# A two-stage sequence kernel on one core: quartered Wq and Wk loads, the adapter's residual turned into the product's bank, x^T added by GpSimd

## The chip, the cores and the metric

The kernel runs on one core of one Trainium2 chip. The metric is the device time of one execution in microseconds. Three runs of the kernel before took 1192.78, 1194.61 and 1195.8 us; the median is 1194.61. The profile is of one further execution, which took 1194.26 us; the span that the profiler shows for its instructions is 1192.5 us.

## What is computed

Four sequences of 512 tokens with 512 features, all in fp32:

```
q, k, v  = x @ Wq, x @ Wk, x @ Wv
attn_out = softmax(q k^T / sqrt(512)) @ v @ Wp + bp
cms      = gelu(attn_out @ cW1 + cb1) @ cW2 + cb2 + one_hot(code)
modifier = gelu(concat(attn_out, cms) @ mW1 + mb1) @ mW2 + mb2
y        = clip(x + cms + modifier, 0, 1)
# adapter, with weights chosen for each sequence by `stream`
h        = gelu(y @ W_down + b_down) @ W_up + b_up
out      = layernorm(y + h) * ln_w + ln_b
```

cW1 is 512 x 2048, cW2 2048 x 512, mW1 1024 x 2048, mW2 2048 x 512; W_down is 512 x 256 and W_up 256 x 512 for each of three experts.

## The kernel before

The four sequences are taken in two pairs. Nearly every product is cut into halves both ways and done with seven products of half size in place of eight (Strassen-Winograd); the large layers do so at two levels, so that an inner product has 128x128 blocks against 256 columns. The sums of blocks that this needs are made on VectorE for the operands, and on GpSimd for the weights. The sums of weights are made once, written to DRAM (`c1_inner`, `c1_outer`, `c2_kept`, `m1_kept`, `m2_kept`) and fetched by SyncE into four buffers `wslot`.

The order of the work is: the head (Wq and Wk turned, and their product W_qk = Wq Wk^T made by `folded`), then for each pair the attention (`pair_product`, `softmax`, `small_product`), and then for each pair the layers c1, c2, m1, m2 (`c1_layer`, `second_layer`, `m1_layer`, `second_layer`) and the adapters. The adapters of the first pair are taken in small steps beside the second pair's c1 layer; those of the last pair run at the end, where sequence 3 goes first and sequence 2 last.

The instructions of an engine stand in the order that a scheduler gives them from the program's order and its own costs; some are held to the program's order by `keep_in_program_order`. Each engine works its queue in order. A buffer that is written again waits for its readers.

The parts that the change touches:

- Head, L123 to L140 and L801 to L805. `weight` loads Wq and Wk in four DMAs of 128 rows each, of 256 KB, taken in turn from SyncE's and ScalarE's queues; x of sequence 0 and Wv follow on ScalarE's queue, x of sequence 1 and Wp on SyncE's. `transposed` turns a whole matrix: 16 transposes into four PSUM banks; then `left_from_psum` and `right_from_psum` copy each bank (ScalarE, L681 and L641) and make the four sums of blocks (VectorE, L516 and L505). `folded` then does the seven products (order 1, 5, 6, 2, 7, 3, 4) of 4 matmuls each, after that x^T of sequence 0 is turned, the biases are turned (`load_bias`, L157), and x^T of sequence 1 is turned with the operands of the first pair product (`both_operands`).
- GpSimd's work in the first 320 us is `expansion`, the sums of weights, with `left_sums` of x (L178 to L181) in between. `late_expansion` does mW2 beside the first pair's m1 layer.
- `second_operands` makes the operands of c2 and m2 from the four blocks of the hidden layer: t1 = h12 - h11, t3 = h22 - h12, t2 = h22 - t1, t4 = h21 - t2, each in a lower and an upper half (`differences`, 128 x 2048 elements, on VectorE). t3 and t4 overwrite h12 and h11. `after(p, g)` is called when product p of the layer before is done for the half g.
- The end of m1, L1418: x^T, kept in DRAM by the attention stage, is added to `cms` by an accumulating DMA from GpSimd's queue for each sequence.
- The adapter, L1293 to L1370. For each sequence: 16 transposes bring y into rows, four banks `res_ps`, ScalarE copies them (L1317) and GpSimd adds b_up (L1318); `down_ps` is two products of 4 matmuls with a gelu each (L1330); then for each of four row tiles two matmuls into `up_ps` (L1335), and VectorE adds the rows (L1343), takes statistics (L1345, L1347), ScalarE takes the root (L1350), and scale and shift follow on ScalarE, VectorE and GpSimd (L1352 to L1368), and a store.

Of the kernel before, what the change touches and what calls it, by code (L numbers as in the profile page):

```python
# [18 lines left out]
def kernel(  # L19
# [103 lines left out]
    wq = weight((nc.sync, nc.scalar, nc.sync, nc.scalar), Wq, slot[0])  # L123
    wk = weight((nc.sync, nc.scalar, nc.sync, nc.scalar), Wk, slot[1])
# [12 lines left out]
    x_rows = [load_x(0, nc.scalar, x_places[0])]  # L137
    wv = weight((nc.scalar, nc.scalar), Wv, slot[2])
    x_rows.append(load_x(1, nc.sync, x_places[1]))
# [34 lines left out]


# [22 lines left out]


# [17 lines left out]
    def expand_c1(u, then):  # L217
# [23 lines left out]
        yield  # L241

# [43 lines left out]
    def expand(unit, raw, pairs, last, then):  # L286
# [46 lines left out]
        else:  # L333
# [3 lines left out]
            yield from plain((1, a11, two), (4, a22, one))  # L337
            yield from full((5, one), (7, three), (6, two))
            then()

    def expand_all(units, raw, pairs, last):
        if last is None:
            load_raw(*units[0][:2], units[0][3], raw)
        for n, unit in enumerate(units):

            def then():
                if n + 1 < len(units):
                    load_raw(*units[n + 1][:2], units[n + 1][3], raw)

            yield from expand(unit, raw, pairs, last, then)  # L350
# [19 lines left out]
    def late_expansion():  # L370

        yield from expand_all(m2_units, slot[6:8], (flat(mod[0]), flat(mod[1]), slot[0]), None)
# [38 lines left out]
    def transposed(get, dst, finish=None):  # L411

        ps = [bank("tr_ps") for d in range(4)]
# [5 lines left out]
        for d in range(4):  # L419
            if finish is None:  # L420
                evacuate(dst[:, d, :], ps[d])
            else:
                finish(d, ps[d])
# [228 lines left out]
    def small_product(lhs, rhs, keep, then=None, copy=nc.scalar.copy):  # L652


        def matmuls(p, _, ps, first_):
# [14 lines left out]
            (1, 5, 6, 2, 7, 3, 4), then, copy,  # L670
# [5 lines left out]
    def left_from_psum(t, s):  # L676

        s1, s2, s3, s4 = (s[:, k] for k in range(4))

        def finish(d, ps):  # L680
            nc.scalar.copy(t[:, d, :], ps)  # L681
            c = d % 2
            if d < 2:
                minus(s3[:, c], ps[:, :256], t[:, c, 256:])
            else:
                minus(s2[:, c], ps[:, 256:], s3[:, c])
                add(s1[:, c], ps[:, 256:], t[:, c, 256:])
                minus(s4[:, c], ps[:, :256], s2[:, c])

        return finish  # L690

    def folded(lhs, rhs, w, s):
# [17 lines left out]
        small_product(lhs, rhs, keep)  # L710
# [71 lines left out]
    def first_operand(pair):  # L782
        xT, t_x = places(pair)
        transposed(chunks(x_rows[2 * pair]), xT[0], right_from_psum(xT[0], sums_in(flat(t_x[0]))))
# [17 lines left out]
    transposed(chunks(wq), wq_t, left_from_psum(wq_t, s_q))  # L802
    transposed(chunks(wk), wk_t, right_from_psum(wk_t, t_k))
    lhs_qk = folded(left_operand(wq_t, s_q), right_operand(wk_t, t_k), w_qk, sums_in(slot[0]))
    first_operand(0)  # L805
    load_bias()
    begun = both_operands(0)
    for pair in range(B // 2):
# [59 lines left out]
        if pair == 0:  # L868
            begun = {}
            then = {6: [lambda: first_operand(1)], 4: [lambda: begun.update(both_operands(1))]}  # L870
# [89 lines left out]
    def c1_operands(slots=(0, 1, 2, 3)):  # L960

        at0, at1, t12, t34 = (in_rows[i] for i in slots)
        b11, b12, b21, b22 = at0[:, 0:2, :], at1[:, 0:2, :], at0[:, 2:4, :], at1[:, 2:4, :]
        t1, t2, t3, t4 = t12[:, 0:2, :], t12[:, 2:4, :], t34[:, 0:2, :], t34[:, 2:4, :]

        def inner_sums(k, t):
            s = mod[1][:, 2 * k : 2 * k + 2, :].rearrange("p a (b n) -> p (a b) n", b=2)
            return inner_operands(t, 1, [s[:, i : i + 1, :] for i in range(4)], pinned=True)
# [4 lines left out]
        one = {1: inner_sums(0, b11)}  # L973
        minus(t1, b12, b11)

        def rest():
            one[5] = inner_sums(1, t1)
# [6 lines left out]
        return one, {2: b21, 3: b22, 4: t4, 6: t2, 7: t3}, rest()  # L984
# [5 lines left out]
    def c1_two_level(p, h, rhs):  # L990
# [3 lines left out]
        for g in range(2):  # L994
            w = next_weights()
            if p == 1:
                for m in range(2):
                    at = m * 512 + g * 256
                    fetch(
                        out=w[:, 512 * m : 512 * m + 512].rearrange("p (c n) -> p c n", c=2),  # L1000
                        in_=cW1[0:256, at : at + 256].rearrange("(c p) n -> p c n", p=P),
                    )
                fetch(out=w[:, 1024:], in_=c1_inner[1, g])
            else:
                fetch(out=w, in_=c1_inner[5, g])
# [17 lines left out]
        def keep(g, place, ps):  # L1023
            o, t = place
            tiles, tokens = slice(4 * o + 2 * g, 4 * o + 2 * g + 2), slice(256 * t, 256 * t + 256)
            nc.scalar.copy(h[2 if p == 1 else 3][:, tiles, tokens], halves_of(ps))
            if p == 1:
                done = h[0][:, tiles, tokens]
                add(done, halves_of(ps), done)
# [5 lines left out]
    def c1_layer(h, rhs, after):  # L1035

        two_level, one_level, rest = rhs
        for p in FIRST_C:
            if p in (1, 5):
                c1_two_level(p, h, two_level[p])  # L1040
                yield
                continue
            for g in range(2):
                w = next_weights()
                if p in (2, 4):
                    k, o = {2: (1, 0), 4: (1, 1)}[p]
# [9 lines left out]
                else:  # L1056
                    s = {3: 2, 6: 0, 7: 1}[p]
                    a = w[:, :1024].rearrange("p (j c n) -> p j c n", j=2, c=2)
                    for j in range(2):
                        fetch(out=a[:, j], in_=c1_outer[j][:, s, g])  # L1060
                    lhs = lambda c, t, a=a: a[:, t // 2, c, (t % 2) * P : (t % 2 + 1) * P]
                for t in range(4):
                    ps = bank(f"c1_{p}")
                    for c in range(2):
                        nc.tensor.matmul(  # L1065
                            ps, lhsT=lhs(c, t), rhs=one_level[p][:, c, :],
# [89 lines left out]
    def second_operands(h):  # L1156
# [19 lines left out]
        def after(p, g):  # L1176

            if (p, g) == (3, 1):
                differences(1, LOW)
                differences(3, LOW)  # L1180
# [4 lines left out]

        ready = []
        return operands, differences, after, ready

    def second_layer(made, src, kept_w, c, last, bias_c, beside):

        operands, differences, _, ready = made
        c11, c12, c21, c22 = c
        rhs = ready[0]
        for i, p in enumerate(SECOND):
# [3 lines left out]
            if i == 0:  # L1198
# [317 lines left out]
```

## Time and profile before

| | |
|---|---|
| median of 3 runs | 1194.61 us |
| profiled execution, its own time | 1194.26 us |
| its span | 1192.5 us |
| TensorE matmuls busy | 1168.9 us, 98% |
| VectorE | 883.5 us, 74% |
| GpSimd | 482.7 us, 40% |
| ScalarE | 294.9 us, 25% |
| chain that ended last | TensorE 92%, DMA 3%, VectorE 2%, GpSimd 2%, ScalarE 1% |
| DMA | 251.50 MB, mean 211 GB/s |
| granted TensorE clock | 0.997 of full |

Times in the profile are microseconds from the start of the span unless they are marked ns. PE is TensorE's matmuls and PEld its weight loads, DVE is VectorE, ACT ScalarE, POOL GpSimd and SP SyncE; a name with a q is the sequencer of that engine, which issues DMAs and waits. A row names the line of the kernel, the engine, the operation, what is written and read, its size and how often; in brackets stands the idle time before it and what ended that. An fp32 matmul shows as two records, a transpose as one. A busy engine costs time only where it is on the chain that ends last; TensorE is on it nearly everywhere, so the question for each stage is whether TensorE stops there and for what.

### The profile page before, as it was taken

Reading aid. Unit: us, or ns where it says so; the run is one execution under the profiler, and the core shown is the slowest. Engines: PE = TensorE matmul, PEld = TensorE weight load, DVE = VectorE, ACT = ScalarE, POOL = GpSimd, SP = SyncE. Lnnn points to the kernel's source line nnn. Section 1 sums busy time; section 2 is a strip of 40 time slices with the busy share of each in tenths; the row PEclk is TensorE's granted clock in tenths of the full one; section 3 lists DMA queues with packets and bytes.
Section 4 is the critical chain, followed back from the end, with each engine's and each line's share of the span. In section 5 each row is a group of like instructions: output and inputs, shape, how many; then the busy total and the mean of one; then the engine's idle time right before and its main releaser. Section 6 shows DMA issues by size and latency. Waiting matters only on the chain.

```text
span 1192.5 us, 13167 instructions
## 1 busy us (share of the span) xinstructions
PE 1168.9 (98%) x4809; PEld 894.8 (75%) x4809; DVE 883.5 (74%) x1221; ACT 294.9 (25%) x540; POOL 482.7 (40%) x542
## 2 busy tenths in 40 slices
PE   7999999999999999999999999999999999999996
PEld 6478558747468888888888857447888888888872
DVE  4735565476789867897899837779894588699947
ACT  3234325335520000012310037551000002220014
POOL 4788999988940048870000522110000010124015
PEclk9999999999999999999999999999999999999998
DMA  8743695698756478787737553132735454775601
GB/s 289 277 149 135 245 351 196 218 389 331 262 194 249 176 279 319 283 293 251 241 134 297 177 177 133 54 132 106 293 131 187 166 211 168 219 240 187 228 1 71
DMA packets 78368, 251.50 MB, mean 211 GB/s; under 512 B 7348, under 2 KB 34016, under 8 KB 63456
## 3 DMA queue, kind: packets, MB, share of 16 engines
q1 hardware_dynamic: 54768, 149.96, 35.0%
q0 software_dynamic: 20736, 89.17, 21.2%
q10 hardware_dynamic: 2800, 11.54, 2.5%
q8 instruction: 38, 0.62, 0.2%
q14 instruction: 26, 0.21, 0.1%
HBM read 185.63 MB, written 65.01 MB: 210 GB/s over the span
## 4 chain that ended last, share of the span: by engine, by line
PE 92%; DMA 3%; DVE 2%; POOL 2%; ACT 1%; SPq 1%; issue 0%; ACTq 0%; DVEq 0%; POOLq 0%
PE i L1215 28%; PE i L1131 27%; PE c L1065 10%; PE sum L595 8%; PE sum L659 7%; PE sum L1014 4%; PE down_ps L1323 2%; PE up_ps L1335 2%; DMA wslot<-c_inner 1%; DMA wslot<-in_L_cond_mW 1%; PE tr_ps L416 1%; PE prod_ps L430 1%; PE res_ps L1314 1%; DMA wide<-in_L_cond_Wk 1%; SPq L988 1%
## 5 line engine op out<-in xcount | busy, mean ns | idle before, releaser
L1131 PE MATMUL i<-slot,wslot 128*128 128x256 f32 x1184 | 260.8, 379 | 0.0
L1131 PEld LDWEIGHTS i<-slot,wslot 128*128 128x128 f32 x1184 | 225.0, 190 | 30.6
L1215 PE MATMUL i<-slot,wslot 128*128 128x256 f32 x896 | 202.5, 379 | 0.0
L1215 PEld LDWEIGHTS i<-slot,wslot 128*128 128x128 f32 x896 | 170.2, 190 | 23.1
L906 ACT COPY first<-i 128x256 f32<-128x256 f32 (+1 forms) x56 | 26.8, 479 | 544.9 <-PE i L1215 280.6
L1215 PE MATMUL i<-hidden,wslot 128*128 128x256 f32 x576 | 132.2, 379 | 0.0
L899 DVE TENSOR_TENSOR part<-i,part 128x512 f32<-128x512 f32 (+1 forms) x156 | 90.9, 591 | 43.1 <-PE i L1131 26.6
L1215 PEld LDWEIGHTS i<-hidden,wslot 128*128 128x128 f32 x576 | 109.4, 190 | 16.2 <-issue 1.4
L928 ACT ACTIVATE hidden<-hidden,bias 128x512 f32<-128x512 f32 x128 | 85.2, 716 | 61.8 <-DVE hidden L505 60.7
L1065 PE MATMUL c<-slot,wslot 128*128 128x512 f32 x224 | 97.3, 592 | 0.0
L1065 PEld LDWEIGHTS c<-slot,wslot 128*128 128x128 f32 x224 | 42.5, 190 | 53.1 <-issue 50.5
L1286 POOL DMA_INDIRECT slot<-in_L_cond_W_down,idx_d x12 | 15.5, 1288 | 149.8 <-PE i L1215 88.2
L1286 POOL DMA_INDIRECT slot<-in_L_cond_b_up,idx_e x3 | 4.3, 1420 | 174.1 <-PE i L1131 173.5
L505 DVE TENSOR_TENSOR sum<-sum,wslot 128x512 f32<-128x512 f32 x51 | 35.4, 697 | 36.8 <-PE sum L659 18.7
L190 DVE TENSOR_TENSOR slot<-hidden,slot 128x1024 f32<-128x1024 f32 x48 | 58.4, 1217 | 0.3
L190 DVE TENSOR_TENSOR slot<-hidden 128x1024 f32<-128x1024 f32 x48 | 58.4, 1216 | 0.0
L899 DVE TENSOR_TENSOR part<-i,first 128x512 f32<-128x512 f32 (+1 forms) x62 | 36.3, 589 | 28.6 <-PE i L1131 16.2
L505 DVE TENSOR_TENSOR hidden<-c,hidden 128x512 f32<-128x512 f32 x64 | 43.3, 688 | 15.5 <-PE c L1065 14.3
L659 PE MATMUL sum<-hidden,wslot 128*128 128x256 f32 x232 | 53.5, 380 | 0.4 <-POOL wslot L180 0.4
L284 POOL DMA_DIRECT2D slot<-in_L_cond_mW x24 | 17.9, 753 | 81.4 <-DVE slot L190 80.5
L659 PEld LDWEIGHTS sum<-hidden,wslot 128*128 128x128 f32 x232 | 43.6, 190 | 6.8 <-POOL wslot L180 0.8
L505 DVE TENSOR_TENSOR hidden<-part,hidden 128x2048 f32<-128x2048 f32 x20 | 48.1, 2405 | 0.5
(307 smaller groups left out, 1988.6 us busy)
## 6 DMA issues: line engine op xcount, KB each, us to landing
wslot<-m_kept SPq DMA_DIRECT2D x48, 1024.0 KB
wslot<-m_kept SPq DMA_DIRECT2D x36, 512.0 KB
wslot<-c_kept SPq DMA_DIRECT2D x16, 1024.0 KB
slot<-in_L_cond_mW POOLq DMA_DIRECT2D x24, 512.0 KB
wslot<-in_L_cond_mW SPq DMA_DIRECT2D x24, 512.0 KB
slot<-in_L_cond_cW POOLq DMA_DIRECT2D x16, 512.0 KB
wslot<-in_L_cond_cW SPq DMA_DIRECT2D x32, 256.0 KB
m_kept<-wide POOLq DMA_DIRECT2D x6, 1024.0 KB
```

What stands on the lines that cost most here:

```text
L190: i = eng.tensor_tensor(out_, one, two, ALU.subtract)
L505: nc.vector.tensor_tensor(dst, a, b, ALU.add)
L595: nc.tensor.matmul(ps, lhsT=lhs[p][:, c, r * P : (r + 1) * P], rhs=rhs[p][:, c, :], start=(first_ and c == 0), stop=(c == 1), skip_group_c ...
L659: nc.tensor.matmul(v[:, j, :], lhsT=lhs[p][:, c, j * P : (j + 1) * P], rhs=rhs[p][:, c, :], start=(first_ and j == 0 and c == 0), stop=(c ...
L899: nc.vector.tensor_tensor(dst, ps, other, ALU.add)
L906: nc.scalar.copy(c1, p1)
L928: nc.scalar.activation(block[:, t, :], block[:, t, :], AF.Gelu, bias=bias_c[:, 8 * half + t : 8 * half + t + 1],)
L1014: nc.tensor.matmul(halves_of(ps)[:, j, :], lhsT=a[g][:, at_[q], j * P : (j + 1) * P], rhs=rhs[q][:, 0, :], start=(first_ and j == 0), stop ...
L1065: nc.tensor.matmul(ps, lhsT=lhs(c, t), rhs=one_level[p][:, c, :], start=(c == 0), stop=(c == 1),)
L1131: nc.tensor.matmul(out_ps[:, j, :], lhsT=a[j][q][:, c, :], rhs=now[q][:, c, :], start=(c == 0), stop=(c == 1),)
L1215: nc.tensor.matmul(ps[:, :256], lhsT=a[k // 2][q][:, k % 2, :], rhs=now[q][:, k, :], start=(k == 0), stop=(k == 3),)
L1323: nc.tensor.matmul(ps, lhsT=wd[:, c, n * P : (n + 1) * P], rhs=y[:, c, :], start=(c == 0), stop=(c == NV - 1),)
```

## The change

Six things change; the diff below is cut to their core.

Head: Wq and Wk are loaded in quarters (256 rows by 256 columns, 256 KB each), Wq's on SyncE's queue and Wk's on ScalarE's; x of sequences 0 and 1, Wv and Wp all follow on SyncE's queue. Fifteen products of a tile of zeros are put ahead on TensorE, and a copy of one column (`touched`) ahead on ScalarE. Each pair of quarters is turned by 8 transposes; product 1 comes after the first pair, the other pairs after product 1, in `folded`, whose order is now 1, 2, 5, 6, 7, 3, 4. The sums are made on 512 columns at a time. x^T of sequence 0 is turned after product 6, and its evacuation follows product 7.

`second_operands`: except in the first pair's c1 layer (`busy`), the lower half of t1 is made of two negations on ScalarE and an accumulating DMA of h12 from GpSimd's queue, and the lower half of t3 follows at the start of the next layer.

c1: the sums for the two products at two levels (p = 1 and 5) are made inside `c1_layer` and no longer before it.

Expansion: in `expand` for mW2, the next unit's loads are asked for before the last three groups of sums, and three steps instead of two go beside each step of m1.

x^T: it is loaded into a buffer (slot 3) and added to `cms` by four GpSimd additions for each sequence, for the first sequence of the pair already inside m1.

Adapter: b_up is gathered as columns and added to y^T by ScalarE (`with_bias`); y^T with it is turned into the bank of the up product, to which the two matmuls are added. Statistics and the first scaling read the bank. The last sequence's down product is cut into token halves, and two row tiles go up before the last quarter of it.

```diff
+    def quarters(src, dst, eng):
+        w = dst.rearrange("p (c n) -> p c n", c=4)
+        for r, k in QUARTERS:
+            rows, columns = slice(256 * r, 256 * r + 256), slice(256 * k, 256 * k + 256)
+            eng.dma_start(
+                out=w[:, 2 * r : 2 * r + 2, columns],
+                in_=src[rows, columns].rearrange("(c p) n -> p c n", p=P),
+            )
+        return w
+    QUARTERS = ((0, 0), (0, 1), (1, 0), (1, 1))
-    wq = weight((nc.sync, nc.scalar, nc.sync, nc.scalar), Wq, slot[0])
-    wk = weight((nc.sync, nc.scalar, nc.sync, nc.scalar), Wk, slot[1])
+    wq = quarters(Wq, slot[0], nc.sync)
+    wk = quarters(Wk, slot[1], nc.scalar)
...
-    x_rows = [load_x(0, nc.scalar, x_places[0])]
-    wv = weight((nc.scalar, nc.scalar), Wv, slot[2])
-    x_rows.append(load_x(1, nc.sync, x_places[1]))
+    x_rows = [load_x(b, nc.sync, x_places[b]) for b in range(2)]
+    wv = weight((nc.sync, nc.sync), Wv, slot[2])
...
+    nc.scalar.copy(touched, eps)
+    nc.vector.memset(zeros, 0.0)
+    idle_ps = bank("idle_ps")
+    for _ in range(15):
+        nc.tensor.matmul(idle_ps[:, :P], lhsT=zeros, rhs=zeros, start=True, stop=True)
...
+    def both_quarters(r, k):
+        of_q, of_k = turned_quarter(wq, r, k), turned_quarter(wk, r, k)
+        place = slice(2 * k, 2 * k + 2), slice(256 * r, 256 * r + 256)
+        nc.scalar.copy(wq_t[:, place[0], place[1]], of_q)
+        if r == 0:
+            nc.vector.tensor_copy(wk_t[:, place[0], place[1]], of_k)
+        else:
+            nc.scalar.copy(wk_t[:, place[0], place[1]], of_k)
+        s1, s2, s3, s4 = (s_q[:, i] for i in range(4))
+        t1, t2, t3, t4 = (t_k[:, i] for i in range(4))
+        if (r, k) == (0, 1):
+            kept_quarters.extend((of_q, of_k))
+        elif (r, k) == (1, 0):
+            minus(t1, of_k, rhs_k[1])
+            minus(s3, lhs_q[1], of_q)
+        elif (r, k) == (1, 1):
+            add(s1, of_q, wq_t[:, 0:2, 256:])
+            minus(s2, of_q, s3)
+            minus(t2, of_k, t1)
...
-    transposed(chunks(wq), wq_t, left_from_psum(wq_t, s_q))
-    transposed(chunks(wk), wk_t, right_from_psum(wk_t, t_k))
-    lhs_qk = folded(left_operand(wq_t, s_q), right_operand(wk_t, t_k), w_qk, sums_in(slot[0]))
-    first_operand(0)
+    ends = []
+    both_quarters(0, 0)
+    lhs_qk = folded(
+        lhs_q, rhs_k, w_qk, sums_in(slot[0]),
+        {
+            1: [lambda r=r, k=k: both_quarters(r, k) for r, k in QUARTERS[1:]],
+            6: [lambda: ends.append(first_operand(0))],
+            7: [lambda: ends[0]()],
+        },
+    )
...
-            if (p, g) == (3, 1):
-                differences(1, LOW)
-                differences(3, LOW)
+            if (p, g) == (3, 0) and not busy:
+                for two in (slice(0, 2), slice(2, 4)):
+                    tc.keep_in_program_order(
+                        nc.scalar.activation(t1[:, two, :], h11[:, two, :], AF.Copy, scale=-1.0)
+                    )
+            elif (p, g) == (3, 1):
+                if busy:
+                    differences(1, LOW)
+                    differences(3, LOW)
+                else:
+                    nc.gpsimd.dma_start(out=t1[:, LOW, :], in_=h12[:, LOW, :], accum_op=ALU.add)
...
+    def up(g, wu, y1, aff, h, t):
+        ps = bank("up_ps")
+        for c in range(NV):
+            nc.tensor.matmul(
+                ps[:, c * P : (c + 1) * P], lhsT=y1[:, c, t * P : (t + 1) * P], rhs=ident,
+                is_transpose=True, start=(c == 0), stop=True, skip_group_check=True,
+            )
+        for n in range(NB):
+            nc.tensor.matmul(
+                ps, lhsT=g[:, n, t * P : (t + 1) * P], rhs=wu[:, n, :],
+                start=False, stop=(n == NB - 1), skip_group_check=True,
+            )
+        stats = small.tile([P, 6], F32, name="stats")
+        nc.vector.bn_stats(stats, ps)
+        mv = small.tile([P, 2], F32, name="mv")
+        nc.vector.bn_aggr(mv, stats)
+        nc.vector.scalar_tensor_tensor(h, ps, mv[:, 0:1], aff[:, 0, :], ALU.subtract, ALU.mult)
+        return mv
...
+    def last_adapter(b, y, loaded, g, rows, y1, eng):
+        wd, wu, bd, bu, aff = loaded
+        with_bias(y, bu, y1)
+        first_half, second_half = slice(0, 256), slice(256, 512)
+        for n, tokens in ((0, first_half), (1, first_half), (0, second_half)):
+            down(y, wd, bd, g, n, tokens)
+        mvs = [up(g, wu, y1, aff, rows[:, t, :], t) for t in range(2)]
+        down(y, wd, bd, g, 1, second_half)
+        for t in range(NT):
+            if t > 1:
+                mvs.append(up(g, wu, y1, aff, rows[:, t, :], t))
+            normalised(b, rows[:, t, :], mvs[t], aff, t, eng, last=True)
...
-        for s in range(2):
-            nc.gpsimd.dma_start(out=cms[s], in_=xT_kept[2 * pair + s], accum_op=ALU.add)
+        def with_input(s, pair=pair):
+            tc.keep_in_program_order(nc.gpsimd.dma_start(out=in_rows[3], in_=xT_kept[2 * pair + s]))
+            for d in range(4):
+                tc.keep_in_program_order(
+                    nc.gpsimd.tensor_tensor(
+                        cms[s][:, d, :], cms[s][:, d, :], in_rows[3][:, d, :], ALU.add
+                    )
+                )
```

## The prediction

> **What bounds the kernel now.** I read the page first (busy time of each engine, the chain that ended last), then the list of waits of TensorE, then the timeline of the first 48 us and of the last 60 us, and last the DMA share by stretches.
>
> The page's busy row (engine, us, share, instructions), then three rows of TensorE's waits (us in total, times, longest):
>
> ```profile
> PE 1168.9 (98%) x4809; PEld 894.8 (75%) x4809; DVE 883.5 (74%) x1221; ACT 294.9 (25%) x540; POOL 482.7 (40%) x542
> ...
> PE i L1131 <- DMA wslot<-in_L_cond_mW: 1.3, 1, 1.3
> PE sum L1014 <- DMA wslot<-c_inner: 1.0, 1, 1.0
> PE sum L595 <- DVE sum L505: 0.9, 1, 0.9
> ```
>
> TensorE is the bound. Paces, from its records: a transpose 0.109 us, a 128x256 matmul two records of 0.216, a 128x512 one two of 0.43. The program's 1164 us of such work in a span of 1192.5 leave some 28 us: the head, the tail, and eight interior stops. Measured from one record's start to the next, less its pace, these are 1.15 us at 42 (VectorE late), 0.64 at 86 and at 191 (softmax), 0.6 at 117 (GpSimd's sums of x, L180), 2.1 around 265 to 269 and 1.6 at 540 (weights not landed), 0.24 at 709, 1.1 at 733 (VectorE again). Only these, the head and the tail can be won; relief of VectorE or ScalarE elsewhere buys nothing.
>
> The head, from the timeline and from the chain (start us, us, what):
>
> ```profile
> 4.39 3.64 PE L416 MATMUL tr_ps<-ident,wide 128*128 128x128 f32 x16 [4.39 <-DMA wide<-in_L_cond_Wq]
> ...
> 8.20 2.92 PE L416 MATMUL tr_ps<-ident,wide 128*128 128x128 f32 x16 [0.16 <-DMA wide<-in_L_cond_Wk]
> 8.82 1.28 ACT L681 ACT_TABLE_LOAD   x1 [8.82 <-DMA wide<-in_L_cond_Wk]
> ```
>
> ```profile
> 12.71 12.41 PE sum L659 x56
> 25.12 1.75 PE tr_ps L416 x16
> 26.87 0.19 PE bias_ps L157
> ```
>
> Sixteen transposes took 3.64 us instead of 1.75: at the start each took 0.213, and only from 10.06 us 0.109. ScalarE issues DMAs until 8.8, then loads its table until 10.11, then copies; the first product starts at 12.71. The place I compare is the bias transpose at 26.87.
>
> The tail, from the timeline:
>
> ```profile
> 1177.79 1.28 ACT L1350 ACT_TABLE_LOAD   x1 [3.00 <-DVE mv L1347]
> ...
> 1184.03 1.56 DVE L1356 SCALAR_TENSOR_TENSOR hidden<-hidden,rstd,wide 128x512 f32<-128x512 f32 x1
> ...
> 1185.51 1.74 DVE L1367 TENSOR_TENSOR hidden<-hidden,wide 128x512 f32<-128x512 f32 x1
> ...
> 1187.29 0.69 DVE L1368 TENSOR_TENSOR hidden<-hidden,wide 128x512 f32<-128x512 f32 x1
> 1188.01 0.33 SPq L1369 DMA_DIRECT2D out<-hidden  x1
> ```
>
> The last matmul ends at 1180.95; VectorE then needs 7 us for four row tiles, and the last store 4.5 us from issue to the span's end.
>
> **What the Trainium skill says.** "TensorE: Matmul & The Clock Gate", Part 1: a cold array runs at half rate until one busy window of a free-running 3.4 us has passed. The trace agrees: half pace from 4.39 to 10.06, 5.7 us, which lies between one window and two. Its section on transposes says that transposes don't warm the array; here nothing else ran, and it warmed. "ScalarE: Activation LUTs", What ACT_TABLE_LOAD costs: about 1.28 us; the trace has 1.28. "SBUF — State Buffer", Who interferes with whom: GpSimd and a VectorE operation with two SBUF inputs exclude each other; the trace agrees in kind (an L190 difference of 0.41 us took 5.46 at 255 with GpSimd busy).
>
> **The change, part by part.**
>
> Head. (a) 15 zero products of 128x128, two records each. VectorE's new memset follows that of eps at 0.80, so they start near 1.1. Cold 0.427 each, warm 0.216. Rate change after 3.4 to 6.8 us of work, taken 5.1: 12 cold (5.1) and 3 warm (0.65), end 6.85; bounds 6.0 and 7.5. (b) First quarter pair: 0.5 MB, which at the 391 GB/s of 3 to 4 us is there at about 4.2, before the zeros end: they hold it. Eight transposes 0.87, to 7.7; ScalarE's copy 0.55 (its table is loaded by `touched` long before) and VectorE's copy 0.69 behind the last transpose: 8.5. Product 1 has 4 matmuls, 1.73: 10.2. (c) The other 24 transposes, 2.6: 12.85. Their data, 2 MB in all, came by about 8.4 before; in runs of 1 KB instead of 2 KB I take at most 9.3, so hidden. (d) Products 2, 5, 6: 5.2, to 18.05. The sums they need are six VectorE operations of 0.69 from 12.8, each ready before its product. x^T's 16 transposes 1.75; x0 now leads SP's queue and lands near 12.5 (16.5 before), hidden. Products 7, 3, 4: 5.2, to 25.0. The bias transpose at 25.05 instead of 26.87: **-1.8** (bounds -2.6 and -1.1 from the zeros' end).
>
> The stop at 42. VectorE worked without pause from 24 to 43.5 there. Now x^T's first eight sums (8 x 0.41 = 3.3 us) are done beside products 3 and 4, before both_operands. From 27.6 its queue holds ten operations of 0.685 and ten of 0.41, 11 us with some waiting 11.6, then two of 0.69 and the sum that product 7 waits for: 41.3. TensorE gets there at 26.9 plus four products of 3.45: 40.7. Stop 0.6 instead of 1.15: **-0.6** (0 to -1.15).
>
> The stop at 117. GpSimd's four sums of x (1.27 each) stand some 4 us earlier in its queue, ahead of cW2 sums and two DMA issues, and x0 lands 4 us earlier: **-0.6** (0 to -0.9).
>
> Around 265 and at 540. Order and bytes of these fetches stay. The DMA share is 0.98 to 1.03 from 236 to 270, filled by GpSimd's expansions. TensorE arrives 3.0 us earlier (1.8 + 0.6 + 0.6); GpSimd, 80 to 100% busy from 100 to 320, starts its list about 4 us earlier for x0's sake, so both sides move: **0** (from -2 to +3).
>
> Layer boundaries, second_operands. For three of four layers t1's lower half (one VectorE operation of 2.4) becomes two ScalarE negations of 1024 elements (estimate 1.0 each from the 0.71 of a 512 ACTIVATE) and a 1 MB accumulating DMA; the lower half of t3, 2.3, moves behind the next layer's first sums and overwrites what that DMA reads, so it waits for it. Behind it stand the evacuations. Before, an accumulating 1 MB DMA (x^T) issued at 551.9 had packets until about 564, 12 us. In the second c1 layer I put the issue at 804, landing 816; VectorE comes to the operation at 811 plus four sums of 1.22, with its backlog 817. No stall; up to 8 banks of 1.73 us each cover TensorE beyond that. TensorE had no stop at these boundaries, so no gain: **0** (0 to +3).
>
> x^T by GpSimd: four accumulating 1 MB DMAs become loads, and 16 additions of 1.27 (rows of that shape). GpSimd only issues DMAs from 533 to 690, the result is wanted three inner products (36 us) later. The lock against VectorE costs it some 5 us a batch, which the 2.4 saved half repay: **0** (0 to +1). The added b_up gathers (16 of one column, about 1.25) run in GpSimd's idle time before 422: 0. The earlier loads of late_expansion leave GpSimd's order as it was: 0.
>
> Adapters in the first c1 layer of the second pair. TensorE's work is the same (64 transposes, 0.109). VectorE per row tile: add 0.69, stats 0.69, aggregate 0.18, scale 0.69, shift 0.2 become stats 0.69, aggregate 0.18, one fused operation 0.98, all from the bank; but p=5's four inner sums (1.7 us in all) move in here. Stops of 1.3 at 709 and 733: **-0.4** (-1.3 to +1).
>
> Tail. TensorE's work, 43.2 us from 1137.7, is unchanged in sum. The second half's gelu ends at 1177.2, table load 1.28: 1178.5, root of tile 0 to 1178.8. VectorE then: reciprocal, stats of tile 2 (0.69), aggregate, reciprocal, fused 0.98, to 1181.3; root 2 comes after two scaled copies of 0.8, 1181.5; final operation of tile 2 beside GpSimd 1.56, to 1183.2; tile 3: stats 0.69, aggregate 0.18, fused 0.98, reciprocal 0.15, final 0.98, with steps between them 1186.3. The store goes out at 1186.6 instead of 1188.0: **-1.4** (-0.8 to -1.9). GpSimd's two additions there replace eight.
>
> Sum: -1.8 - 0.6 - 0.6 - 0.4 - 1.4 = **-4.8**. The profiled execution took 1194.26 (span 1192.5 and 1.8 around it), 0.35 under the median of the three runs, 1194.61. On the median: 1189.8.
>
> **Rivals.** *Given back at the full DMA* (20%): if GpSimd's expansions do not move earlier with x0, TensorE meets the same landing at 269 and waits 3.0 longer: only tail and adapters remain, -1.8, 1192.8, no measurable change. For it: shares of 1.0 up to 270. Against: GpSimd's first wait was for x0 (16.54, 10.79 us idle).
> *Slower by late weights* (9%): the additional megabyte at each of three boundaries delays SP's weight transfers. The price is that of 540, where stores on the GpSimd queue cost 1.6; the gain is eaten at 1.6 per boundary, and from 2.8 each it is over 0.3% slower: 1198.5. Against: the share was 0.52 to 0.76 from 560 to 620.
> *All stops close* (16%): no stop at 42, 117, 709, 733, the zeros warm early, the tail at its bound: -2.6 - 1.15 - 0.9 - 1.3 - 1.9 = -7.9: 1186.7.
> *The zeros do nothing for the clock*: then product 1 and the transposes run cold; 8 transposes, product 1 and 24 transposes cost 5.2 more from 7.5, and the head loses 4: inside the no-change case (5 of its 20%).
>
> **How the numbers follow.** Likeliest (55%): 1189.8, own range 1187.5 to 1191.5. Faster by over 0.3% (3.6 us, about what a measurement of this kernel can tell from no change), that is below 1191.0: 47 of these 55 and the 16: 0.63, and part of the give-back, 0.05: 0.68. Within: 8 of the 55 and 15 of the 20, 0.23. Slower: 0.09. Range for 8 in 10: 1186.0 to 1194.0; outside lie the late weights and the far end of the closed stops.
>
> **What would show it.** Right: bias transpose at about 25; transposes after 7 us at 0.109; no stop at 117; last store issued some 6 us earlier than before by the span's clock; no new stop near 823, 600 or 1065. Wrong: a VectorE wait for a DMA in the t3 difference, TensorE waiting for wslot at a boundary, a stop of over 4 us at 265.

## The result

The changed kernel takes 1190.05 us (median of 16 runs, 1186.76 to 1194.32); the kernel before, run beside it, takes 1192.92 (16 runs, 1189.35 to 1197.35). The ratio is 0.9975, with a 95% interval of 0.9961 to 0.9989: 2.9 us faster. The interval leaves out 1, so the gain is real, but it is inside the 0.3% that the forecast called no measurable change, and to which it gave 0.23. The forecast was 4.8 us, from a base of 1194.61; over more runs the base itself came down by 1.7, so the forecast of 1189.8 meets the measured time with a smaller gain than it stood for. That the two times agree to 0.3 us is luck.

The profiled execution of the changed kernel happens to be the slowest of its 16, 1194.32 us, with a span of 1192.5 as before. A second profile of the same kernel (called after_again below) has a span of 1188.4 and a time of 1190.15, the median. Both are used, because where they differ is part of the answer.

The page's busy row of the first profile, to be put beside that of before:

```profile
PE 1173.3 (98%) x4855; PEld 902.3 (76%) x4855; DVE 865.2 (73%) x1187; ACT 301.6 (25%) x546; POOL 499.7 (42%) x555
```

TensorE's waits of the same profile (us in total, times, longest):

```profile
PE i L1217 <- DMA wslot<-in_L_cond_mW: 5.1, 1, 5.1
PE sum L1087 <- DMA wslot<-in_L_cond_cW: 2.1, 1, 2.1
...
PE sum L700 <- POOL wslot L201: 1.1, 1, 1.1
PE sum L700 <- DVE hidden L849: 0.9, 1, 0.9
```

The reader sees three of the old stops, at 540, 265 and 117, all as long or longer than before, and the one at 42 gone. The zeros add 30 records to TensorE's work, 3.3 us at the pace of 0.109.

The head, from the timeline (start us, us, what):

```profile
1.08 5.88 PE L193 MATMUL idle_ps<-zeros 128*128 128x128 f32 x30 [1.08 <-DVE zeros L190]
6.80 1.04 PE L836 MATMUL tr_ps<-ident,wide 128*128 128x128 f32 x8
8.71 1.97 PE L700 MATMUL sum<-hidden 128*128 128x256 f32 x8 [0.88 <-DVE hidden L849]
10.51 2.78 PE L836 MATMUL tr_ps<-ident,wide 128*128 128x128 f32 x24
```

and from the chain, the place that the forecast compared:

```profile
25.41 0.18 PE bias_ps L168
```

Zeros to 6.96, product 1 at 8.7, bias transpose at 25.4: the head is as forecast to half a microsecond.

The tail, from the timeline:

```profile
1180.91 1.28 ACT L1458 ACT_TABLE_LOAD   x1
...
1184.83 4.57 SPq L1467 DMA_DIRECT2D out<-hidden  x4
1185.01 1.56 DVE L1463 SCALAR_TENSOR_TENSOR hidden<-hidden,rstd,wide 128x512 f32<-128x512 f32 x1
...
1187.43 0.75 DVE L1452 SCALAR_TENSOR_TENSOR hidden<-up_ps,mv,wide 128x512 f32<-128x512 f32 x1
...
1188.29 0.75 DVE L1463 SCALAR_TENSOR_TENSOR hidden<-hidden,rstd,wide 128x512 f32<-128x512 f32 x1
```

The last matmul starts at 1184.10 here and at 1180.52 before; both spans end at 1192.5. So the tail, from that start to the span's end, is 3.5 us shorter (8.44 against 11.96), and TensorE reaches it 3.6 us later: the whole gain of the tail is spent above it. In after_again the last matmul starts at 1179.92, and the tail is 8.45.

To see where it is spent I compared the start of the same matmul record in both traces, the records being counted from the first (without the 30 of zeros). The number is how far TensorE is ahead (-) or behind (+) the kernel before, in us:

| place (us in before) | after | after_again | tail alone | head alone | x_accum | sums_dve |
|---|---|---|---|---|---|---|
| 27.6, after the head | -1.5 | -2.2 | -1.0 | -1.7 | -1.6 | -1.2 |
| 100, after the stop at 42 | -2.6 | -3.3 | -1.0 | -2.8 | -2.8 | -3.0 |
| 224, after the stop at 117 | -2.2 | -2.4 | -0.9 | -2.0 | -2.5 | -3.9 |
| 300, after the stop at 265 | -1.8 | -1.5 | -0.9 | -0.9 | -1.2 | -5.1 |
| 560, in m1 | +4.3 | +0.1 | -0.5 | +0.5 | +0.5 | -5.5 |
| 690, before the adapters | +4.7 | +0.5 | -0.5 | +1.4 | +4.8 | -5.1 |
| 1000, after the adapters | +3.7 | -0.5 | -1.9 | +1.4 | +3.9 | -6.0 |
| last matmul to span's end, less that of before | -3.5 | -3.5 | -3.8 | 0.0 | -3.5 | -3.5 |

Tail alone, which has the old head, is 1.0 ahead at 27.6 too, and the two other kernels with the old head, described below, are 0.9 (old_head) and 0.5 (tail_xt) ahead: the profile of before has the slowest of four old heads. The ten profiles with the new head are 1.1 to 2.4 ahead, 1.1 more on the mean than the four. Each column is one execution, and its head can be off by as much as this.

In after and after_again a lead of 2.6 to 3.3 us at 100 has turned into a lag by 600. The two profiles lose it in different ways. In the first, weights of m1 land late and the clock falls afterwards. By stretches (PE busy is the first figure after the length, the granted clock stands before the DMA share):

```profile
530.00:540.00 10.00, 8.69 (x41) 7.30 (x39) 9.79 (x12) 2.56 (x4) 1.83 (x4) 1.00 1.03 424
540.00:550.00 10.00, 6.21 (x18) 5.10 (x19) 3.37 (x3) 3.04 (x5) 2.49 (x2) 0.66 0.64 270
```

The stop is 5.3 us, and the eleven records after it run at half pace, 2.4 us more. In the second profile there is no stop at 540; VectorE is late at 505 instead. TensorE's waits of after_again, and VectorE's operation at 490 from its timeline:

```profile
PE i L1217 <- DVE part L970: 2.4, 3, 1.3
...
PE sum L700 <- POOL wslot L201: 1.6, 1, 1.6
```

```profile
490.60 11.57 DVE L544 TENSOR_TENSOR hidden<-part,hidden 128x2048 f32<-128x2048 f32 x1
```

In the first profile the same operation took 3.66 us. GpSimd's timeline shows what VectorE's difference met, first profile and then second:

```profile
491.97 4.15 POOL L326 TENSOR_TENSOR wide<-slot 128x1024 f32<-128x1024 f32 x1 [0.23 <-DMA m_kept<-wide]
```

```profile
492.04 2.34 POOL L326 TENSOR_TENSOR wide<-slot 128x1024 f32<-128x1024 f32 x1
```

In the first, GpSimd waited 0.23 us for a store, VectorE's difference went ahead, and GpSimd's own operation took 4.15 instead of 2.34. In the second, without that gap, six more GpSimd operations started and ended before VectorE got its turn, near 500. The gap is not what decides, though: before, tail_xt and sums_dve have none there, and VectorE went ahead all the same. In tail_xt, VectorE and then GpSimd:

```profile
491.29 3.60 DVE L505 TENSOR_TENSOR hidden<-part,hidden 128x2048 f32<-128x2048 f32 x1
```

```profile
492.69 4.41 POOL L298 TENSOR_TENSOR wide<-slot 128x1024 f32<-128x1024 f32 x1
```

What lets VectorE in at that point stays open.

In after_again TensorE then stops 3.2 us in all at 505 to 520; GpSimd is through its list six microseconds earlier, and the weights at 540 are in time.

### The profile page after: what moved, and what is told of

It reads as the page before. It is cut to its first block, busy times and chain, and to the rows that moved or that the text cites. A ratio compares the mean times of both kernels' runs of the same rounds, so it can differ in the third digit from the quotient of the medians.

```text
span 1192.5 us, 13251 instructions
## 1 busy us (share of the span) xinstructions
PE 1173.3 (98%) x4855; PEld 902.3 (76%) x4855; DVE 865.2 (73%) x1187; ACT 301.6 (25%) x546; POOL 499.7 (42%) x555
## 4 chain that ended last, share of the span: by engine, by line
PE 86%; POOL 5%; DMA 5%; issue 1%; DVE 1%; ACT 1%; SPq 0%; POOLq 0%; DVEq 0%
PE i L1315 28%; PE i L1217 26%; PE c L1151 10%; PE sum L634 6%; PE sum L700 5%; PE sum L1087 4%; DMA wslot<-in_L_cond_mW 3%; PE down_ps L1421 2%; PE up_ps L1440 2%; DMA wslot<-in_L_cond_cW 1%; DMA c_outer<-part 1%; PE tr_ps L451 1%; POOL wide L198 1%; PE up_ps L1435 1%; PE idle_ps L193 0%
## 5 line engine op out<-in xcount | busy, mean ns | idle before, releaser
L1539 POOL DMA_DIRECT2D slot<-xT_kept x4 | 2.9, 722 | 171.7 <-PE i L1217 171.7
L1542 POOL TENSOR_TENSOR cms<-cms,slot 128x512 f32<-128x512 f32 x16 | 21.9, 1390 | 81.8 <-PE i L1217 59.7
L1217 PE MATMUL i<-cms,wslot 128*128 128x256 f32 x192 | 45.3, 385 | 5.1 <-DMA wslot<-in_L_cond_mW 5.1
```

The costliest lines, as they stand in the source:

```text
L1217: nc.tensor.matmul(out_ps[:, j, :], lhsT=a[j][q][:, c, :], rhs=now[q][:, c, :], start=(c == 0), stop=(c == 1),)
```

## The experiments

Each kernel ran beside the kernel before, in four sets. The medians of the kernel before were 1193.06 us (set of after_again, x_accum, x_late and sums_early), 1192.22 (tail_alone, head_alone, busy_all, old_expansion), 1192.74 (old_head, tail_xt, sums_dve) and 1192.56 (sums_dve_plain). Between sets the ratios to it compare more safely than the times. In the diffs the changed kernel is the old side, unless another is named.

First theory: x^T's load, which stands 20 us earlier than the accumulating DMA and right behind two stores, causes the stop at 540.

**after_again**: no edit.

> The changed kernel itself, once more with its profile, beside the kernel before. Theory (x^T too early): the stop of TensorE at 540 us, 1.6 us in the kernel before and 5.3 us in the changed one, comes from the 1 MB load of x^T, issued at 531.3 behind two stores of 1 MB; it is there in every execution, 4 to 6 us, with some ten records at half pace behind it. Rival (chance): the profiled execution was the slowest of 16, and here the stop is 1 to 3 us and the clock stays up. Time 1189 to 1191 in either case, ratio 0.996 to 0.999.

1190.15 us (21 runs), ratio 0.9971 (0.9961 to 0.9982). No stop at 540. So the long stop is not in every execution; but the chance theory missed the 3.2 us at 505 to 520 that stand in its place.

**x_accum**:

```diff
-            if i == 10:
-                with_input(0)
...
-        with_input(1)
+        for s in range(2):
+            nc.gpsimd.dma_start(out=cms[s], in_=xT_kept[2 * pair + s], accum_op=ALU.add)
```

> The changed kernel with x^T added again by an accumulating DMA behind the m1 layer, as in the kernel before; all else as changed. Theory (x^T too early): the stop at 540 falls back to 1 to 2 us with no slow records behind it, and the time falls by 3 to 6 us against the changed kernel run beside it, to 1184 to 1187. Rival (chance, or the stores of the sums for mW2 alone): stop and time stay within 1 us of the changed kernel's.

1196.61 us (15 runs), ratio 1.0030 (1.0013 to 1.0047): 6.5 us more than the changed kernel, where the theory had 3 to 6 less. The theory fell. TensorE's lead tells where: it is like after_again to 588, then loses 4.2 us at 590 and 4.2 at 1057, the two boundaries of m1 and m2. The timeline there:

```profile
573.76 0.85 POOL L1275 DMA_DIRECT2D wide<-hidden  x1 [20.45 <-ACT wide L1268]
...
576.65 0.85 POOL L1553 DMA_DIRECT2D cms<-xT_kept  x1 [2.03 <-PE i L1217]
577.24 2.67 SPq L415 DMA_DIRECT2D wslot<-in_L_cond_mW  x2
...
592.47 14.01 PE L1217 MATMUL i<-slot,wslot 128*128 128x256 f32 x56 [2.31 <-DMA wslot<-in_L_cond_mW]
```

Two accumulating megabytes, the boundary's and x^T's, leave within 3 us just ahead of the weights, which TensorE then waits for; at both places the clock falls too (nearly half of each loss). This is what the "late weights" rival of the forecast described, brought about by two such transfers together. The changed kernel escapes it because x^T is loaded earlier for one sequence and added by GpSimd.

**x_late**:

```diff
             if i == 10:
+                gate = small.tile([P, 1], F32, name="gate")
+                tc.keep_in_program_order(nc.gpsimd.tensor_copy(gate, part[:, 0, 0:1]))
                 with_input(0)
```

> The changed kernel with the GpSimd additions of x^T kept, but the first load of x^T held back until the eleventh half of m1 is written (some 35 us later) by a copy of one column on GpSimd. Theory (x^T too early): the moment of the load is what costs, not the additions: the stop at 540 falls to 1 to 2 us and the time to 1184 to 1187, as with the accumulating DMA. Rival (the additions cost through the lock with VectorE): no gain, or 1 to 3 us worse than the accumulating DMA.

1192.81 us (14 runs), ratio 0.9995 (0.9982 to 1.0007), 2.7 us more than the changed kernel. Stops of 1.4 to 1.9 at 592 and of 2.0 at 1057 are there again, and 505 to 520 is as in after_again. The later the load, the nearer to the boundary's DMA. What I had taken for the cause is what keeps the boundary free.

**sums_early**: the sums of x of sequence 1 in `wslot[3]`, asked for ahead.

```diff
-        s_x = [sums_in(wslot[k]) for k in (2, 0)]
+        s_x = [sums_in(wslot[k]) for k in (2, 3)]
...
-            left_sums(x_rows[s1], s_x[1])
+        left_sums(x_rows[s1], s_x[1])
```

> The changed kernel with the sums of x of sequence 1 in a weight buffer that is free, asked for at the start of the attention instead of behind the first softmax. Theory: the stop at 117 (1.2 us in the changed kernel) is GpSimd's sums standing behind the sums of weights, which wait for a store to land; it disappears, and the products behind it come 1 us earlier up to 224 us. Of that the weights at 265 take back up to all. Time 0 to 1.2 us below the changed kernel run beside it. Rival (TensorE waits there for something else as well): the stop stays at 0.5 us or more.

That buffer was not free: the pair products keep intermediate sums in it, so this kernel computes other values for the attention. 1193.41 us (14 runs), ratio 1.0005 (0.9991 to 1.0019). The stop at 117 is gone and one of 6.2 us stands at 32, where TensorE waits for that buffer. As a test of the stop's worth it is spoilt.

Second theory: the gain is the tail's, the head's is given back.

**tail_alone**: the kernel before with `load_adapter` to `last_adapter`, `spaces` and the calls of the changed one.

```diff
-        for t in range(NT):
-            ps = bank("res_ps")
...
+        mv = up(g, wu, y1, aff, rows[:, t, :], t)
...
+            adapt(0, spaces[0], nc.sync, kind=last_adapter)
```

> The kernel before with the changed adapters alone (b_up as columns, residual turned into the bank, the last down product in token halves); head, layers and x^T as before. Theory (the gain is the tail's): from the last matmul's start to the span's end it was 12.0 us before and 8.4 to 8.5 in two profiles of the changed kernel, so the time falls by 3.0 to 4.2 us here, ratio 0.9965 to 0.9975, as much as the whole change gives. Rival (the forecast's sum): 1.8 us for tail and adapters, ratio 0.9985, the other half of the gain coming from the head.

1188.07 us (6 runs), ratio 0.9947 (0.9926 to 0.9968): 4.2 us faster by the medians, 6.3 by the ratio (3.8 to 8.8), at the far end of what the theory gave or beyond it, and no less than the whole change gives. In the profile the tail gives 3.8, and the stop of VectorE at 733 disappears with the lighter adapters (1.4 between 690 and 815).

**head_alone**: the kernel before with `quarters`, `zeros`, `both_quarters`, the order of `folded` and `begin_transposed`.

```diff
-    wq = weight((nc.sync, nc.scalar, nc.sync, nc.scalar), Wq, slot[0])
+    wq = quarters(Wq, slot[0], nc.sync)
...
-    transposed(chunks(wq), wq_t, left_from_psum(wq_t, s_q))
+    both_quarters(0, 0)
```

> The kernel before with the changed head alone (quarters, zeros, touched, order of loads, evacuation of x^T of sequence 0 behind product 7). Theory (given back): TensorE is 2.5 to 3.5 us earlier at 100 us, waits that much longer for GpSimd at 117, at the weights of 265 and in m1, and the time falls by 0 to 1.2 us, ratio 0.999 to 1.000. Rival (the forecast's sum): 3.0 us faster, ratio 0.9975.

1194.60 us (22 runs), ratio 1.0015 (1.0003 to 1.0026): slower, where the forecast had 3.0 faster and the theory 0 to 1.2. Its waits of TensorE:

```profile
PE i L1193 <- DMA wslot<-in_L_cond_mW: 2.8, 1, 2.8
PE sum L1076 <- DMA wslot<-in_L_cond_cW: 2.2, 1, 2.2
PE sum L691 <- POOL wslot L203: 1.4, 1, 1.4
```

Each of the three places takes back more than it did before: the lead goes from 2.8 to 2.0, 0.9 and then below zero.

**busy_all**:

```diff
-        made = second_operands(h, pair == 0)
+        made = second_operands(h, True)
...
-        made = second_operands(h)
+        made = second_operands(h, True)
```

> The changed kernel with the differences of second_operands made on VectorE at all four boundaries, that is without the three negations on ScalarE and the accumulating 1 MB DMAs; x^T still by GpSimd. Theory (the DMA at the boundary collides with weights, the difference on VectorE is hidden): the short stop at 590 (0.3 us) goes, no other comes, the time is that of the changed kernel or up to 1 us less. Rival (VectorE's 4.7 us per boundary were on the path): 1 to 4 us more than the changed kernel, with VectorE waits of TensorE at 600, 823 and 1065.

1189.29 us (10 runs), ratio 0.9958 (0.9941 to 0.9975). No VectorE stop at the boundaries, and none at 590: the theory holds as to the trace. As a time, 0.9 us less than the changed kernel is not distinguishable from nothing; the profiled execution, at 1197.05 us, is far above the median, and its stops at 115 and 543 are long.

**old_expansion**:

```diff
-            then()
             yield from full((5, one), (7, three), (6, two))
+            then()
...
-                steps(between, 3)
+                steps(between, 2)
```

> The changed kernel with the list of the sums for mW2 as before: the next loads asked for behind the last sums, two steps and not three beside each step of m1. Theory (GpSimd's uninterrupted list shuts VectorE out): in the second profile of the changed kernel one VectorE difference of 128x2048 took 11.6 us at 490 and TensorE then stopped 3.2 us at 505 to 520; with the old list GpSimd has its gaps again, that difference takes 3 to 5 us, the stop at 505 goes, and that of 540 for weights (1.5 us) comes back: 0 to 2 us below the changed kernel. Rival: the lock is there with either list, time within 0.7 us of the changed kernel's.

1189.86 us (22 runs), ratio 0.9980 (0.9968 to 0.9992), the changed kernel's. The profile has the difference of 11.62 us and the stops at 505 to 520 as in after_again: the rival was right, the new order of the list is not what shuts VectorE out.

Third: does the head do anything in company, and is GpSimd what takes it back?

**old_head**: the changed kernel with the head of before, the reverse of head_alone's edit.

```diff
-    wq = quarters(Wq, slot[0], nc.sync)
+    wq = weight((nc.sync, nc.scalar, nc.sync, nc.scalar), Wq, slot[0])
...
-    both_quarters(0, 0)
+    transposed(chunks(wq), wq_t, left_from_psum(wq_t, s_q))
```

> The changed kernel with the head of the kernel before: whole matrices turned, loads of rows, no zeros; all else as changed. Theory (the head's gain is given back and its earlier arrival costs at the weights): TensorE is 3 us later at 100 us, waits less at 117, 265 and in m1, and the time is 0 to 2 us below the changed kernel: 1187.5 to 1190, near the tail alone. Rival (the forecast's sum): 3 us above it, 1193.

1190.25 us (22 runs), ratio 0.9983 (0.9971 to 0.9994). The changed kernel has 1190.15 and, by the ratio, 0.9971 (0.9961 to 0.9982): the new head in company is worth 0.1 us by the medians and 1.4 by the ratios, and the intervals overlap, so it can't be told from nothing. The forecast's sum would have 1193, a ratio of 1.000, outside the interval. old_head also lies 2.2 us above tail_alone, from which it differs by the boundaries, the c1 sums, x^T and the list; the intervals don't meet.

**tail_xt**: tail_alone with `with_input` of the changed kernel.

```diff
-        for s in range(2):
-            nc.gpsimd.dma_start(out=cms[s], in_=xT_kept[2 * pair + s], accum_op=ALU.add)
+            if i == 10:
+                with_input(0)
...
+        with_input(1)
```

> The kernel before with the changed adapters and with x^T loaded and added by GpSimd; differences at the boundaries on VectorE, list of sums and head as before. Theory (x^T's load only pays where an accumulating DMA stands at the boundary): within 1.5 us of the tail alone, 1186.5 to 1189.5, with the stop at 540 of 2 to 4 us if the load is issued behind the two stores at 531. Rival (x^T by GpSimd is a gain by itself, as the loss of 6.5 us with the accumulating DMA suggests): 3 us or more below the tail alone, 1185 or less.

1186.97 us (6 runs), ratio 0.9952 (0.9934 to 0.9970), the same as tail_alone. Its profile has no stop at 540 at all, with x^T's load issued at 532.3 behind two stores, just as in the changed kernel. So the load there does not by itself bring that stop (the stop of 2 to 4 us that was expected did not come), and x^T by GpSimd costs nothing that these runs can tell, but is no gain by itself. old_head, of the same set, lies 3.3 us above, so its loss is not x^T's.

**sums_dve**:

```diff
-                left_sums(x_rows[s1], s_x[1])
+                weight_sums(*halves(x_rows[s1]), *(s_x[1][:, i] for i in range(4)), nc.vector)
```

> The changed kernel with the four sums of x of sequence 1 on VectorE instead of GpSimd. Theory (given back at the full DMA): the stop at 117, 1.2 to 2.9 us in the profiles so far, is gone, TensorE is that much earlier at 224, and the stops around 265 and in m1 grow by as much: time within 1 us of the changed kernel, 1189 to 1191. Rival (the stop at 117 is what eats the head's gain): 1.2 to 2.5 us below it, 1187.5 to 1189.

1187.49 us (6 runs), ratio 0.9949 (0.9931 to 0.9967). As to the trace the rival was right and more: the stop at 117 is gone, and the stops behind it did not grow, they shrank. As to the time, the interval reaches up to 0.9967 and the changed kernel's down to 0.9961, so they overlap; the profiled execution took 1184.58 us, among the shortest of the six. Its waits:

```profile
PE i L1217 <- DMA wslot<-in_L_cond_mW: 1.0, 1, 1.0
...
PE sum L1087 <- DMA wslot<-in_L_cond_cW: 0.8, 1, 0.8
```

In this profile TensorE keeps the head's 3 us and is 5.1 ahead at 300. The four sums were 5.1 us of GpSimd's list; without them GpSimd issues the loads that follow at 112.6 instead of 116.8 (in after_again), and the stores that fill the DMA ahead of 265 about 2 us earlier (the last at 250.1 instead of 252.2), while SyncE's c1 weights go out at 249.9 instead of 252.6.

**sums_dve_plain**: both the last edit and busy_all's two lines.

> The changed kernel with both: the four sums of x of sequence 1 on VectorE, and all differences of second_operands on VectorE. Theory (GpSimd's list is late by these sums, and the accumulating DMA at the boundary only adds traffic): no stop at 117, under 1.2 us at 265, none at 590; 0 to 1 us below the sums on VectorE alone, 1186.5 to 1187.5, and 2.5 to 3.5 us below the changed kernel. Rival (what VectorE takes over twice is too much for it): VectorE stops near 600 or 823, 1189 or more.

1187.68 us (11 runs), ratio 0.9957 (0.9940 to 0.9974): no gain over sums_dve. The stops at 117 and 590 are gone and that at 265 is small again (1.1 in two), but VectorE stops TensorE once near 74 (1.1 us), and the difference at 488 took 8.9 us, with 3.4 us of stops at 502 to 518.

tail_alone, tail_xt and sums_dve have the best medians, 2.1 to 3.2 us below the changed kernel's, each with 6 runs. tail_alone's interval reaches up to 0.9968 and the changed kernel's down to 0.9961, so the two overlap slightly; among the three nothing is told apart.

## Why the prediction came out as it did

By its own steps; "after" and "after_again" give the measured pair.

- **Head, -1.8**: right in its mechanism, -1.5 and -2.2 against the one profile of before. As that has the slowest of four old heads, the head is worth nearer 1.1. Product 1 at 8.7 (forecast 8.5), transposes done at 13.3 (12.85), bias at 25.4 (25.05). That the zeros do nothing for the clock is refuted: the transposes from 6.80 run at 0.109.
- **Stop 42, -0.6**: mechanism right, size too small: the stop is gone, -1.15 in both.
- **Stop 117, -0.6**: wrong, +0.45 and +0.95. The step said that GpSimd's sums stand 4 us earlier. GpSimd is 3 us earlier up to 82.4, but its next operation waits for the store of `part` to land, 8.5 us instead of 6.2, and starts at 91.7 instead of 92.4. TensorE arrives 2.6 earlier and waits for the last of the four sums, which ends at 117.1. sums_dve shows that these sums are the stop. GpSimd's operation behind that wait, before and after:

```profile
92.38 2.36 POOL L298 TENSOR_TENSOR part<-slot,slot 128x1024 f32<-128x1024 f32 x1 [6.20 <-DMA c_outer<-part]
```

```profile
91.66 2.37 POOL L326 TENSOR_TENSOR part<-slot,slot 128x1024 f32<-128x1024 f32 x1 [8.51 <-DMA c_outer<-part]
```

- **Around 265, 0**: +0.35 and +0.9, inside its bounds. "Both sides move" came true in the main: TensorE is 2.2 and 2.4 ahead at 224, and the last two stores of GpSimd ahead of this place start 2.1 and 2.8 earlier (252.35 and 251.66 instead of 254.50). What landed in time for TensorE moved by a little less than TensorE did.
- **540, 0**: the step that failed most: +6.5 and +1.9 over all of m1 to 600. "Order and bytes of these fetches stay" is true, and it was not enough: TensorE's earlier arrival meets either a landing that comes no earlier (in the first profile TensorE goes on at 543.8 instead of 541.9), or VectorE shut out by GpSimd. Which of the two comes depends on whether VectorE gets in at 490, and each cost more here than the 1.6 of before. I looked at the stop as one fixed price of one execution.
- **Layer boundaries, 0**: no new stop of more than 0.4 at 600, 823 and 1065. But the step counted its two DMAs one by one. x_accum shows that two accumulating ones together cost 8 us in its profile; only the edit of x^T keeps the boundary's DMA harmless, and no run shows a gain from the pair. The share of 0.52 to 0.76 that spoke against late weights was a mean over 20 us: in stretches of 10 us, 560 to 570 has 0.97 and 580 to 590 has 0.88.
- **x^T by GpSimd, 0**: right, by tail_xt.
- **Adapters in c1, -0.4**: -0.95 in both. The 1.2 us at 733 go; 0.5 us appears at 716, where product 5's inner sums moved in (TensorE waits there for a VectorE sum in both profiles, and not in tail_alone, which gains 1.4).
- **Tail, -1.4**: right in kind, mis-sized: -3.5 in both. VectorE's end, measured from the last matmul's start, moved by 2.5 (7.45 to 4.94) and not by 1.4. Three operations that I had put at 0.98 took 0.73 to 0.75, two of them out of PSUM and the last one out of SBUF, with nothing on GpSimd beside it; that is 0.7 of the 1.1. The 0.98 came from an operation at 1182.94 that ran beside GpSimd's additions, and so was no price of its own. And the span ends 3.5 us after the last store's issue instead of 4.5; before, two stores left within 0.85 us of each other, but whether that is the reason was not tested.

The sum -4.8 was thus -1.5 - 1.15 + 0.45 + 0.35 + 6.5 - 0.95 - 3.5 = +0.2 in the first profile and -2.2 - 1.15 + 0.95 + 0.9 + 1.9 - 0.95 - 3.5 = -4.05 in the second (spans: 0.0 and -4.1). The 20% rival, *given back at the full DMA*, describes what happened to the head better than the likeliest case did: in these two profiles all of it is given back, only later and dearer than at 269, and by the times of old_head most or all of it. The tail's error of 2 us in the other direction covered for it, and that is luck. Not settled: which part of the boundaries, c1 sums and list costs the 2.2 us between old_head and tail_alone; x^T is not it (tail_xt), the stop at 716 is 0.5 of it, and one at 1052 in old_head 0.3. Nor what lets VectorE in at 490, nor why the weights at 540 land at different times: those issued at 526.8 landed 9.4 us later in tail_xt, and those issued at 527.0 in old_head 14.3 us later, with the same issues ahead of them.

## To carry to other kernels

A head start for the engine that bounds is worth only what the next late producer lets through: look for that producer's list (here GpSimd's 5 us of sums) and shorten it first, because taking work off it made the stop behind it smaller too in both profiles that show it, though the times don't yet tell the kernels apart. The end of a kernel has no such filter, and what is won behind the last matmul is kept. Two extra transfers that are harmless alone should be priced together when they are issued within one weight fetch of each other, and a stop read from one profile should be looked at in a second before it is given a price.

## What was not expected of the hardware

- **An accumulating DMA takes over twice the DMA time of a load.** Share of the 16 engines in the 40 us from 560 to 600, GpSimd's queue (packets, MB, share), in busy_all (one plain load of x^T), before (accumulating alone) and x_accum (accumulating, over two):

```profile
q0 software_dynamic: 144, 1.05, 6.3%
```

```profile
q0 software_dynamic: 208, 1.44, 18.4%
```

```profile
q0 software_dynamic: 339, 2.38, 32.2%
```

  That is 2.4, 5.1 and 5.4 us of all 16 engines per MB. SyncE's plain fetches took 2.7 to 2.8 us per MB in each of the three stretches, so it is not the company that made the difference.
- **VectorE can be passed over by several GpSimd instructions.** The Trainium skill, "SBUF — State Buffer", Who interferes with whom, says that the ports which VectorE and GpSimd share are an exclusive lock, and that the order of issue decides who blocks. The traces agree, and add that VectorE, when it is shut out, can miss its turn at several GpSimd operations in a row: 8.9 to 11.6 us for the 128x2048 difference near 490 in five of the fourteen profiles, 3.2 to 4.4 in the other nine, three of which have no gap in GpSimd's list there either. VectorE's operation with one input from PSUM and one from SBUF was not slowed: at 1183.75 in after it took 0.73 beside GpSimd's addition, where the one at 1185.01 with both from SBUF took 1.56, and 0.75 at 1188.29 with GpSimd idle.
- **Short stops can cool the clock.** "TensorE: Matmul & The Clock Gate", Part 1, has the array go cold after at least one idle window of about 3.4 us. Here stops of 1.9 (1057, x_accum), 2.3 (264, x_late), 2.5 (590, x_accum) and 2.9 us (115, busy_all) were followed by eight to fourteen records at half pace, 1.7 to 3.1 us each time; stops of 2.0 (1057, x_late), 2.3 (263, after), 2.8 (115, x_late), 2.9 (115, old_expansion, and 539, head_alone) and 3.6 (542, sums_early) were not. The three longer ones all were (4.7 in busy_all, 5.3 in after, 6.2 in sums_early). So a stop of 2 to 3 us may cost nearly its double here, below the window that the page states, and it does so in some profiles and not in others.
